# A two-layer graph network on one core: another order of the setup, and other buffers, banks and a queue for the adjacency

## The chip, the cores and the metric

The kernel runs on one core of one Trainium2 chip. The metric is the device time of one execution in microseconds (us); lower is better. A core has TensorE (PE; its weight loads are listed apart as PEld), VectorE (DVE), ScalarE (ACT), GpSimd (POOL) and SyncE (SP, here only a queue for DMAs). Each works through its own list of instructions in order, and semaphores make one wait for another.

## The reference

Eight graphs of 2048 nodes with 256 features share one 2048 x 2048 adjacency. Two layers follow each other; cut to what matters:

```python
# layer 0: h = relu(layernorm(x)); attention in 8 chunks of 256 keys, each with a softmax of its own
q, k, v = (h @ Wq.T + bq, h @ Wk.T + bk, h @ Wv.T + bv)       # 4 heads of 64
scores = clip(q . k / 8, -10, 10);  scores = where(adj == 0, -10, scores)
ctx = sum over chunks of softmax(scores in the chunk) @ v
x = x + layernorm(ctx @ Wo.T + bo + h) * gamma + beta
# layer 1: h = relu(layernorm(x)) again, called g here
h = g @ W;  e = leaky_relu(h . a1 [row] + h . a2 [column], 0.01)
x = x + relu(softmax(where(adj == 0, -1e9, e)) @ h)
```

## The kernel before

**Work.** The program is written out for each of the 8 graphs: a stretch of attention (32 steps: 4 blocks of 512 queries by 8 chunks of 256 keys), then the second layer. Before the first graph's attention stands a setup, once in the whole kernel; the changed code is in it, and in three helpers that it calls.

**Order.** `tc.manual_schedule` keeps the order of the source on all five engines, so the order of the calls is the order of each engine's list. A tile of a pool has a tag; a tag has a fixed number of buffers, and a new tile waits until a buffer's last user is done. A piece of work that waits holds up all that is behind it on its engine.

**Setup.** Four blocks of 512 rows of the first graph are loaded (`load`, SP), given statistics (`stats`, DVE), `power` (ACT) and `shift` (DVE: the last term of the norm), normed (`norm`, ACT, two halves), transposed (`turn`: TensorE, then a copy by DVE for half c = 0 and by ACT for c = 1), and projected: `qk(nb, 0)` gives q, `qk(nb, 1)` gives k (TensorE, then copies by ACT), `values` gives v (TensorE, then DVE). `turn_weight` transposes a weight on TensorE and copies it on DVE.

**Adjacency.** Beside that, the first 24 of the adjacency's 32 parts of 128 x 1024 are turned into "bounds", int8 values that serve as upper clip of the scores (the last 8 parts are done during the attention, by `adjacency`). For part i, `load_rows` brings 512 KB of int32 (four buffers; `find(i)` issues the load of part i + 4). `find` (`missing_of`, L211) compares with zero on DVE and gives z, in bf16. `bound` (`turn_missing`, L218, then `keep_bounds`) transposes z on TensorE in eight pieces to a bank of PSUM, and ACT scales it to int8. Parts 0 to 15 go to resident bounds of blocks 0 and 1; parts 16 to 23 go to a tile `bound_part`, and from there by a DMA of 128 KB to HBM (`bound_d`, runs of 128 bytes).

**PSUM.** Eight banks: tag "s" two tiles of two banks, "n" two of one bank, "t" two of one bank. In the setup `ps_m` takes "n" and "t" in turn, counting in `turn_about`; z's transposes take "t".

**SBUF tags that matter.** "hn" (5 buffers: normed halves, raw weights, and z), "e" (5: the attention's exponentials), "r" (2: `bound_part` in the setup; later a row of the second layer), "o4" and "prod" (1 each: output and product of the attention, both first used when the attention runs).

**The end of the setup.** `Attention.early` starts step 0 of the attention: part 0 the logits of its first two heads (they need block 0 of q and k alone), part 1 their clips (DVE) and exponentials (ACT) and the other heads' logits, part 2 clips, an exponential and a sum `add(0, 0)` of exponentials on GpSimd, part 3 the next step's first logits. After that `begin` and `end` run a step each: `begin(2)` holds the exponential of step 0's last head and `add(0, 1)`; `end(2)` holds the values matmuls (L427) and the sums matmuls (L439), which read both `add`s. On GpSimd's list stand these adds (L466) and, from the second chunk on, the DMAs that accumulate the context (L486). SP's list goes on, behind the setup's row loads, with the output weight (L190), the second layer's weight (L973), two stores of 1 MB of bounds (L129) and the next two parts' rows.

In the names of the setup, the loop before the change is:

```python
    for nb in range(NNB - 1):
        proj.norm(nb + 1, 0)
        proj.qk(nb, 0, ps_h)
        bound(6 * nb, 6 * nb + 1)
        proj.norm(nb + 1, 1)
        ...
        find(6 * nb + 2, 6 * nb + 3)
        proj.qk(nb, 1, ps_h)
```

Of the kernel before, what the change touches and what calls it, by code (L numbers as in the profile page):

```python
# [9 lines left out]
BF16 = mybir.dt.bfloat16  # L10
I32 = mybir.dt.int32
I8 = mybir.dt.int8
# [5 lines left out]
P = 128  # L18
# [10 lines left out]
def gnn_two_layers(  # L29
# [18 lines left out]
    nc = tc.nc  # L48
# [8 lines left out]
    NNB = N // NB  # L57
# [8 lines left out]
    ps = ctx.enter_context(tc.tile_pool(name="ps", bufs=2, space=PSUM))  # L66
# [11 lines left out]
    turn_about = [False, 0]  # L78

    def ps_m():  # L80
        if turn_about[0]:
            turn_about[1] += 1
            if turn_about[1] % 2:
                return ps_n()
        return ps_t()
# [8 lines left out]
    work = ctx.enter_context(tc.tile_pool(name="work", bufs=2, reuse_waits="tile"))  # L94
# [11 lines left out]
    wqT = const.tile([P, FC, F], F32, name="wqT")  # L106
    wkT = const.tile([P, FC, F], F32, name="wkT")
    wvT = const.tile([P, FC, F], F32, name="wvT")
# [6 lines left out]
    bound_d = [kept.tile([P, NT, NB], I8, name=f"bound_d{nb}") for nb in range(NNB)]  # L115
# [25 lines left out]
    def row_bcast(src, name):  # L141
        t = const.tile([P, F], F32, name=name)
        nc.sync.dma_start(t, row(src))
        return t
# [50 lines left out]
    def turn_weight(raw, wT):  # L195
        pt = ps_m()
        for di in range(FC):
            for do in range(FC):
                k = di * FC + do
                nc.tensor.transpose(pt[:, k * P:(k + 1) * P], raw[:, do, di * P:(di + 1) * P], ident)  # L200
        nc.vector.tensor_copy(wT.rearrange("p c f -> p (c f)"), pt)

    HALF = N // 2

    def load_rows(t, half):
        rows = xpool.tile([P, HALF], I32, tag="x", name="rows", bufs=NNB)
        nc.sync.dma_start(rows, adj[t * P:(t + 1) * P, half * HALF:(half + 1) * HALF])
        return rows

    def missing_of(rows, t, half):  # L210

        z = work.tile([P, HALF], BF16, tag="hn", name="z", bufs=5)
        nc.vector.tensor_scalar(
            z, rows, 0.0, 0.0, op0=ALU.is_equal, op1=ALU.add, accum_out=missing[:, t, half:half + 1]
        )
        return z

    def turn_missing(z):  # L218
        pt = ps.tile([P, 8, P], BF16, tag="t", name="ps_z")
        for k in range(8):  # L220
            nc.tensor.transpose(pt[:, k, :], z[:, k * P:(k + 1) * P], ident_b)
        return pt

    def keep_bounds(pt, t, half):

        nb, rows, cols = t // TB, slice(half * 8, (half + 1) * 8), slice((t % TB) * P, (t % TB + 1) * P)
        if nb in bounds:
            dst = bounds[nb][:, rows, cols]
        else:
            dst = work.tile([P, 8, P], I8, tag="r", name="bound_part")  # L230
        nc.scalar.activation(dst, pt, AF.Copy, scale=-2.0 * CLIP * SC, bias=CLIP * SC)
        if nb not in bounds:
            nc.scalar.dma_start(bound_d[nb][:, rows, cols], dst)

    def find_lone():
        nc.vector.tensor_reduce(lone, missing, AX.X, ALU.add)
# [4 lines left out]
    def adjacency(parts):  # L241


        def load(i):
            rows[i] = load_rows(*parts[i])

        def find(i):
            found[i] = missing_of(rows.pop(i), *parts[i])

        def turn(i):  # L250
            found[i] = turn_missing(found[i])

        def keep(i):
            keep_bounds(found.pop(i), *parts[i])

        finds = [9, 11, 15, 17, 21, 23, 29, 31]
        turns = [12, 12, 18, 18, 26, 26, 32, 32]
        todo = {}
        for i, (f, t) in enumerate(zip(finds, turns)):
            todo.setdefault(f - 6, []).append(lambda i=i: load(i))  # L260
            todo.setdefault(f, []).append(lambda i=i: find(i))
            todo.setdefault(t, []).append(pe(lambda i=i: turn(i)))
            todo.setdefault(t + 1, []).append(first(lambda i=i: keep(i)))
        return todo
# [628 lines left out]
    proj = Projection(0)  # L893
    turn_about[0] = True
    raws = {}
# [9 lines left out]
    rows = {i: load_rows(*nearest[i]) for i in range(4)}  # L905
    proj.stats(0, range(TB))
    proj.power(0)
    for name, wT in (("q", wqT), ("k", wkT), ("v", wvT)):
        turn_weight(raws[name], wT)
    proj.shift(0)  # L910
    proj.norm(0, 0)
    proj.norm(0, 1)
    proj.load(2)
# [4 lines left out]
    def find(*parts):  # L918
        for i in parts:
            found[i] = missing_of(rows.pop(i), *nearest[i])  # L920
            if i + 4 < len(nearest):
                rows[i + 4] = load_rows(*nearest[i + 4])

    def bound(*parts):
        for i in parts:
            keep_bounds(turn_missing(found.pop(i)), *nearest[i])

    find(0, 1)
    for nb in range(2):
        bounds[nb] = bound_tile()  # L930
    proj.stats(1, range(TB))
    proj.power(1)
    proj.shift(1)
    for nb in range(NNB - 1):
        proj.norm(nb + 1, 0)
        proj.qk(nb, 0, ps_h)
        bound(6 * nb, 6 * nb + 1)
        proj.norm(nb + 1, 1)
        if nb + 3 < NNB:
            proj.load(nb + 3)  # L940
        find(6 * nb + 2, 6 * nb + 3)
        proj.qk(nb, 1, ps_h)
        bound(6 * nb + 2, 6 * nb + 3)
        proj.turn(nb + 1, 0)
        proj.turn(nb + 1, 1)
        find(6 * nb + 4, 6 * nb + 5)
        if nb + 2 < NNB:
            proj.stats(nb + 2, range(TB))
            proj.power(nb + 2)
            proj.shift(nb + 2)  # L950
        proj.values(nb)
        bound(6 * nb + 4, 6 * nb + 5)
        if nb == 0:
            bo_r = row_bcast(bo, "bo_r")
            gamma_r = row_bcast(gamma, "gamma_r")
            beta_r = row_bcast(beta, "beta_r")
        find(6 * nb + 6, 6 * nb + 7)
    proj.qk(NNB - 1, 0, ps_h)
    att = Attention(proj)
    att.early(0)  # L960
    bound(18, 19)
    proj.qk(NNB - 1, 1)
    find(20, 21)
    att.early(1)
    bound(20, 21)
    find(22, 23)
    proj.values(NNB - 1)
    att.early(2)
    bound(22, 23)
    att.early(3)  # L970

    def layer1_weight():
        nc.sync.dma_start(w1s[:, :, 0:F], w1.rearrange("(c p) f -> p c f", p=P))  # L973
# [26 lines left out]
    for b in range(B):  # L1000
# [208 lines left out]
        for i, (nb, j4) in enumerate(pieces1):  # L1209
# [21 lines left out]
            if far and i in (1, 3, 6, 9):  # L1231
                n = (1, 3, 6, 9).index(i)
# [3 lines left out]
            if ahead and i == len(pieces1) - 4:  # L1236
                att = Attention(ahead)
# [38 lines left out]
```

## Time and profile before

| | us |
|---|---|
| median of 3 runs | 3614.5 |
| lowest, highest | 3611.58, 3620.66 |
| the profiled execution, whole | 3618.74 |
| its span, first to last instruction | 3616.9 |

| engine | busy us (share of the span) |
|---|---|
| PE | 3579.6 (99%) |
| DVE | 2583.1 (71%) |
| ACT | 1960.0 (54%) |
| POOL | 1787.0 (49%) |

The setup and the first step's start fill about the first 98 us of the span. In that stretch PE is busy for 76.89 us, DVE for 54.38, ACT for 51.82 and POOL for 3.23. A wait in the profile reads "who <- whom: total us, times, longest"; a row of a stretch gives its length, then the busy time of PE, PEld, DVE, ACT and POOL with the count of instructions, then the granted clock of TensorE, the DMA engines' share and GB/s.

### The profile page before, as it was taken

To read this page: it belongs to the slowest core of one execution; us is meant where nothing else is said; L and a number is where in the kernel's file an instruction comes from. 1 tells how busy PE (TensorE), PEld (TensorE's weight loads), DVE (VectorE), ACT (ScalarE), POOL (GpSimd) and SP (SyncE) were. 2 spreads that over 40 slices of the span, in tenths; PEclk is the share of its full clock that TensorE was granted. 3 is DMA by queue.
4 is the path that set the end of the run, shared out by engine and by line. 5 is a ranking of instruction groups with operands and counts; after the bars stand their busy time and mean duration, and the time that the engine had idled before them with its cause. 6 is when DMAs were issued, how large, how long until landed. Compare 5 with 4: busy or idle time off the path is not lost.

```text
span 3616.9 us, 104751 instructions
## 1 busy us (share of the span) xinstructions
PE 3579.6 (99%) x46544; PEld 2222.8 (61%) x46544; DVE 2583.1 (71%) x3919; ACT 1960.0 (54%) x2975; POOL 1787.0 (49%) x1138
## 2 busy tenths in 40 slices
PE   8999999999999999999999999999999999999999
PEld 4444785547855577555775558755586555865568
DVE  5888577865778667786677866677666785767866
ACT  5677416774167742677326772367723677137650
POOL 0678016870168702786027860378503784047841
PEclk9999999999999999999999999999999999999999
DMA  6444213341133412344113432134322343114321
GB/s 216 118 107 101 53 56 82 79 110 38 56 84 84 112 30 73 78 92 93 46 58 84 101 77 62 48 84 101 72 62 59 78 95 74 53 48 90 78 57 46
DMA packets 149430, 283.61 MB, mean 78 GB/s; under 512 B 39664, under 2 KB 104944, under 8 KB 140784
## 3 DMA queue, kind: packets, MB, share of 16 engines
q0 software_dynamic: 32256, 117.45, 17.7%
q1 hardware_dynamic: 100080, 157.36, 13.7%
q8 instruction: 364, 5.96, 0.7%
q10 hardware_dynamic: 16640, 2.10, 0.4%
q14 instruction: 90, 0.74, 0.1%
HBM read 138.41 MB, written 21.02 MB: 44 GB/s over the span
## 4 chain that ended last, share of the span: by engine, by line
PE 97%; DMA 1%; DVE 1%; ACT 1%; issue 0%; POOL 0%; ACTq 0%; SPq 0%; DVEq 0%; POOLq 0%
PE ps_s L411 24%; PE ps_n L427 24%; PE ps_s L856 12%; PE ps_t L439 6%; PE ps_n L856 6%; PE ps_t L856 6%; PE ps_t L635 2%; PE ps_t L355 2%; PE ps_n L355 2%; PE ps_s L355 2%; PE ps_n L714 2%; PE ps_t L714 1%; PE ps_t L369 1%; PE ps_n L369 1%; PE ps_t L302 1%; DMA ctxT<-prod 1%
## 5 line engine op out<-in xcount | busy, mean ns | idle before, releaser
L466 POOL TENSOR_TENSOR both<-e 128x1024 f32<-128x1024 f32 x512 | 1216.3, 2402 | 639.3 <-PE ps_t L439 340.8
L451 DVE SCALAR_TENSOR_TENSOR e<-ps_s,bound 128x1024 f32<-128x1024 f32 x1024 | 1225.0, 1221 | 412.1 <-PE ps_s L411 410.2
L411 PE MATMUL ps_s<-q,k 64*32 64x512 f32 x16384 | 1412.0, 590 | 2.1 <-DVE e L451 2.1
L460 ACT ACTIVATE e<-e 128x1024 f32<-128x1024 f32 x1024 | 1050.3, 1050 | 466.5 <-DVE e L451 447.9
L427 PE MATMUL ps_n<-e,v 64*32 64x512 f32 x16384 | 1206.8, 590 | 4.1 <-ACT e L460 2.2
L427 PEld LDWEIGHTS ps_n<-e,v 64*32 64x32 f32 x16384 | 456.6, 107 | 479.8 <-issue 397.2
L411 PEld LDWEIGHTS ps_s<-q,k 64*32 64x32 f32 x16384 | 454.2, 106 | 453.1 <-issue 343.9
L874 POOL TENSOR_TENSOR x<-x,r 128x256 f32<-128x256 f32 x124 | 95.7, 772 | 1104.1 <-DVE rz L866 997.3
L439 PE MATMUL ps_t<-both,ones 64*32 64x512 f32 x4096 | 534.6, 590 | 0.1
L856 PE MATMUL ps_s<-g,w 128*128 128x257 f32 x2048 | 447.3, 380 | 0.0
L856 PEld LDWEIGHTS ps_s<-g,w 128*128 128x128 f32 x2048 | 388.4, 190 | 56.0
L481 DVE TENSOR_TENSOR prod<-ps_n,rz 128x512 f32<-128x512 f32 x448 | 288.7, 686 | 166.3 <-PE ps_n L427 96.6
L839 DVE SCALAR_TENSOR_TENSOR w<-bound,w 128x1024 f32<-128x1024 int8 x256 | 313.7, 1225 | 8.7
L856 PE MATMUL ps_n<-g,w 128*128 128x257 f32 x1024 | 292.4, 382 | 0.0
L856 PE MATMUL ps_t<-g,w 128*128 128x257 f32 x1024 | 289.7, 380 | 0.0
L471 ACT ACTIVATE rz<-ps_t 128x512 f32<-128x512 f32 x256 | 152.6, 596 | 229.8 <-PE ps_t L439 185.7
L833 DVE TENSOR_SCALAR w<-src,cd 128x512 f32<-128x512 f32 x512 | 265.3, 561 | 10.7 <-ACT src L827 6.9
L486 POOL DMA_DIRECT2D ctxT<-prod x224 | 192.3, 859 | 57.8 <-DVE prod L481 55.5
L856 PEld LDWEIGHTS ps_n<-g,w 128*128 128x128 f32 x1024 | 192.8, 190 | 44.3 <-issue 17.6
L856 PEld LDWEIGHTS ps_t<-g,w 128*128 128x128 f32 x1024 | 193.8, 189 | 28.2
L275 ACT ACTIVATE krn<-mv,eps 128x4 f32<-128x4 f32 x32 | 9.5, 296 | 292.7 <-DVE mv L271 292.7
L472 ACT ACTIVATE rz<-rz 128x512 f32<-128x512 f32 x256 | 161.4, 630 | 8.2
(125 smaller groups left out, 2953.3 us busy)
## 6 DMA issues: line engine op xcount, KB each, us to landing
ctxT<-prod POOLq DMA_DIRECT2D x224, 512.0 KB, 4.8
bound<-bound_d SPq DMA_DIRECT2D x62, 1024.0 KB, 5.7
xp<-in_x_dram SPq DMA_DIRECT2D x60, 512.0 KB, 5.7
rows<-in_adj_dram SPq DMA_DIRECT2D x32, 512.0 KB, 5.2
x<-in_x_dram SPq DMA_DIRECT2D x32, 512.0 KB, 5.3
out_dram<-x SPq DMA_DIRECT2D x31, 512.0 KB, 2.9
src<-source_d SPq DMA_DIRECT2D x24, 256.0 KB, 5.0
bound_d<-bound_part ACTq DMA_DIRECT2D x16, 128.0 KB, 4.3
```

The lines of the kernel that those rows point to most:

```text
L355: nc.tensor.matmul(pp, w[:, di, do * P:(do + 1) * P], self.hT[nb][:, di, :], start=di == 0, stop=di == FC - 1,)
L411: nc.tensor.matmul(self.s[n, o][c * Q:(c + 1) * Q, kt, :], self.k[p][rows, at:at + Q], self.q[p][rows, nb * NB:(nb + 1) * NB], start=True, ...
L427: made.append(nc.tensor.matmul(self.num[n, c][h * Q:(h + 1) * Q, :], self.v[rows, j * KT + kt, at:at + Q], self.e[n, p][rows, i * KT + kt, :],
L439: nc.tensor.matmul(self.total[n][h * Q:(h + 1) * Q, :], ones[rows, :], self.both[n, h // 2][rows, h % 2, :], start=half == 1, stop=half == 0,)
L451: nc.vector.scalar_tensor_tensor(self.e[n, p][:, i * KT:(i + 1) * KT, :], self.s.pop((n, o)), -CLIP * SC, bounds[nb][:, j * KT:(j + 1) * K ...
L460: nc.scalar.activation(e, e, AF.Exp, scale=1.0 / SC)
L466: nc.gpsimd.tensor_tensor(self.both[n, p], e[:, 0], e[:, 1], op=ALU.add)
L481: nc.vector.tensor_tensor(dst[:, c, :], self.num.pop((n, c)), self.rz[n], op=ALU.mult)
L486: nc.gpsimd.dma_start(self.ctxT[nb], self.prod.pop(n), accum_op=ALU.add)
L833: nc.vector.tensor_scalar(w[:, i, :], self.src[nb], self.cd[:, 0, j:j + 1], self.cd[:, 1, j:j + 1], op0=ALU.mult, op1=ALU.max,)
L839: nc.vector.scalar_tensor_tensor(two, bounds1[nb][:, j - 1:j + 1, :], 0.0, two, op0=ALU.is_gt, op1=ALU.mult)
L856: nc.tensor.matmul(accs[t][:, 0:F + 1], w[:, i, t * P:(t + 1) * P], g[:, j, :], start=j == 0, stop=j == NT - 1,)
```

## The change

- In the setup z is put in a buffer of tag "e" and not "hn" (`in_setup`, set to False when the setup is written out).
- A bound that goes to HBM takes a buffer of tag "r", "o4", "r" or "prod" by part: parts 16, 18, 20, 22 "r" (two buffers), 17 and 21 "o4", 19 and 23 "prod". Its DMA is issued from GpSimd and not from ACT.
- While `turn_about` is on, z's transposes take "n" and "t" in turn, in one count with `ps_m`.
- The order: block 0's `shift` stands ahead of the copies of the k and v weights; block 1's statistics and shift stand ahead of finds 0 and 1; in the loop, finds stand ahead of bounds, both norms of a block stand one block earlier behind the transposes (block 1's after q of block 0), the next block's statistics ahead of the transposes; `early(0)` stands ahead of block 3's q, which now takes "n" and "t"; the values of block 3 stand behind all bounds.

```diff
@@ -201,6 +201,9 @@
         nc.vector.tensor_copy(wT.rearrange("p c f -> p (c f)"), pt)
 
     HALF = N // 2
+    in_setup = [True]
+
+    part_tags = ["r", "o4", "r", "prod"]
 
     def load_rows(t, half):
         rows = xpool.tile([P, HALF], I32, tag="x", name="rows", bufs=NNB)
@@ -209,14 +212,20 @@
 
     def missing_of(rows, t, half):
 
-        z = work.tile([P, HALF], BF16, tag="hn", name="z", bufs=5)
+        tag = "e" if in_setup[0] else "hn"
+        z = work.tile([P, HALF], BF16, tag=tag, name="z", bufs=5)
         nc.vector.tensor_scalar(
             z, rows, 0.0, 0.0, op0=ALU.is_equal, op1=ALU.add, accum_out=missing[:, t, half:half + 1]
         )
         return z
 
     def turn_missing(z):
-        pt = ps.tile([P, 8, P], BF16, tag="t", name="ps_z")
+        tag = "t"
+        if turn_about[0]:
+            turn_about[1] += 1
+            if turn_about[1] % 2:
+                tag = "n"
+        pt = ps.tile([P, 8, P], BF16, tag=tag, name="ps_z")
         for k in range(8):
             nc.tensor.transpose(pt[:, k, :], z[:, k * P:(k + 1) * P], ident_b)
         return pt
@@ -227,10 +236,12 @@
         if nb in bounds:
             dst = bounds[nb][:, rows, cols]
         else:
-            dst = work.tile([P, 8, P], I8, tag="r", name="bound_part")
+            tag = part_tags[(2 * t + half) % 4] if in_setup[0] else "r"
+            dst = work.tile([P, 8, P], I8, tag=tag, name="bound_part", bufs=2 if tag == "r" else 1)
         nc.scalar.activation(dst, pt, AF.Copy, scale=-2.0 * CLIP * SC, bias=CLIP * SC)
         if nb not in bounds:
-            nc.scalar.dma_start(bound_d[nb][:, rows, cols], dst)
+            queue = nc.gpsimd if in_setup[0] else nc.scalar
+            queue.dma_start(bound_d[nb][:, rows, cols], dst)
 
     def find_lone():
         nc.vector.tensor_reduce(lone, missing, AX.X, ALU.add)
@@ -905,9 +916,10 @@
     rows = {i: load_rows(*nearest[i]) for i in range(4)}
     proj.stats(0, range(TB))
     proj.power(0)
-    for name, wT in (("q", wqT), ("k", wkT), ("v", wvT)):
-        turn_weight(raws[name], wT)
+    turn_weight(raws["q"], wqT)
     proj.shift(0)
+    turn_weight(raws["k"], wkT)
+    turn_weight(raws["v"], wvT)
     proj.norm(0, 0)
     proj.norm(0, 1)
     proj.load(2)
@@ -925,49 +937,54 @@
         for i in parts:
             keep_bounds(turn_missing(found.pop(i)), *nearest[i])
 
-    find(0, 1)
     for nb in range(2):
         bounds[nb] = bound_tile()
     proj.stats(1, range(TB))
     proj.power(1)
     proj.shift(1)
+    find(0, 1)
     for nb in range(NNB - 1):
-        proj.norm(nb + 1, 0)
+        i = 6 * nb
         proj.qk(nb, 0, ps_h)
-        bound(6 * nb, 6 * nb + 1)
-        proj.norm(nb + 1, 1)
-        if nb + 3 < NNB:
-            proj.load(nb + 3)
-        find(6 * nb + 2, 6 * nb + 3)
+        if nb == 0:
+            proj.norm(1, 0)
+            proj.norm(1, 1)
+            proj.load(3)
+        find(i + 2, i + 3)
+        bound(i, i + 1)
         proj.qk(nb, 1, ps_h)
-        bound(6 * nb + 2, 6 * nb + 3)
-        proj.turn(nb + 1, 0)
-        proj.turn(nb + 1, 1)
-        find(6 * nb + 4, 6 * nb + 5)
+        find(i + 4, i + 5)
+        bound(i + 2, i + 3)
         if nb + 2 < NNB:
             proj.stats(nb + 2, range(TB))
             proj.power(nb + 2)
             proj.shift(nb + 2)
+        proj.turn(nb + 1, 0)
+        proj.turn(nb + 1, 1)
+        if nb + 2 < NNB:
+            proj.norm(nb + 2, 0)
+            proj.norm(nb + 2, 1)
         proj.values(nb)
-        bound(6 * nb + 4, 6 * nb + 5)
+        find(i + 6, i + 7)
+        bound(i + 4, i + 5)
         if nb == 0:
             bo_r = row_bcast(bo, "bo_r")
             gamma_r = row_bcast(gamma, "gamma_r")
             beta_r = row_bcast(beta, "beta_r")
-        find(6 * nb + 6, 6 * nb + 7)
-    proj.qk(NNB - 1, 0, ps_h)
     att = Attention(proj)
     att.early(0)
+    proj.qk(NNB - 1, 0)
+    att.early(1)
+    find(20, 21)
     bound(18, 19)
     proj.qk(NNB - 1, 1)
-    find(20, 21)
-    att.early(1)
+    att.early(2)
     bound(20, 21)
     find(22, 23)
+    bound(22, 23)
     proj.values(NNB - 1)
-    att.early(2)
-    bound(22, 23)
     att.early(3)
+    in_setup[0] = False
 
     def layer1_weight():
         nc.sync.dma_start(w1s[:, :, 0:F], w1.rearrange("(c p) f -> p c f", p=P))
```

## The prediction

> **What bounds the kernel now.** I read the page's first two parts first, then stretches by engine, then waits and the chain inside the first 100 us.
>
> ```profile
> PE 3579.6 (99%) x46544; PEld 2222.8 (61%) x46544; DVE 2583.1 (71%) x3919; ACT 1960.0 (54%) x2975; POOL 1787.0 (49%) x1138
> PE   8999999999999999999999999999999999999999
> ```
>
> TensorE is busy in every slice but the first. So only the first slice, where the changed code runs, can move: what TensorE saves there is saved at the end, and nothing else is. I cut that slice at the starts of the four q projections and of the first values matmul that runs on (98.5), with 200 us of the later work below:
>
> ```profile
> 13.15:34.50 21.35, 16.74 (x89) 10.66 (x89) 13.49 (x34) 11.54 (x21) 0.00 (x0) 0.98 0.69 237
> 34.50:53.40 18.90, 15.72 (x91) 10.08 (x89) 10.61 (x24) 11.48 (x18) 0.00 (x0) 0.93 0.53 179
> 53.40:70.20 16.80, 16.00 (x92) 10.13 (x90) 9.01 (x17) 10.11 (x15) 0.00 (x0) 0.90 0.48 159
> 70.20:98.50 28.30, 22.68 (x200) 10.68 (x196) 16.41 (x22) 14.63 (x17) 2.35 (x1) 1.00 0.81 222
> 200.00:400.00 200.00, 199.96 (x3231) 104.01 (x3218) 151.24 (x231) 148.19 (x234) 140.70 (x91) 1.00 0.40 92
> ```
>
> Columns: length, then busy time of PE, PEld, DVE, ACT, POOL, then TensorE's clock, DMA share, GB/s. No engine is full in the four stretches; in-order waits make them long. TensorE's waits from 13 to 98.6, and two of the others:
>
> ```profile
> PE ps_z L221 <- DVE v L374: 4.8, 2, 2.4
> PE ps_t L302 <- ACT bound L231: 2.4, 3, 0.8
> PE ps_n L427 <- ACT e L460: 2.2, 1, 2.2
> PE ps_s L411 <- DVE e L451: 2.1, 2, 1.1
> PE ps_s L355 <- ACT q L359: 1.4, 1, 1.4
> ACT krn L275 <- DVE mv L271: 17.6, 4, 5.1
> ```
>
> The first: a second transpose of the adjacency needs bank "t" of the value that VectorE has not yet read, since VectorE stands behind finds and statistics. The last stretch, from the chain:
>
> ```profile
> 84.44 1.02 ACT bound_part L231
> 85.46 0.02 issue
> 85.48 8.85 DMA bound_d<-bound_part
> 94.33 0.02 issue
> 94.35 0.02 ACTq L231
> ```
>
> A bound leaves for HBM through one of two buffers; the next waits for the landing (8.85 us), and the exponentials stand behind it on ScalarE.
>
> **What the skill says.** "TensorE: Matmul & The Clock Gate", Part 1: idleness halves the clock, and some microseconds of work restore it. The trace agrees: after the 2.4 us waits the q matmuls start 0.85 apart and not 0.43, at clock 0.93 and 0.90 above. "SBUF — State Buffer", Who interferes with whom: `tensor_scalar` with an accumulator does not lock GpSimd out. The finds are that form, 1.22 us for 1024 elements; no run here shows it beside a GpSimd DMA. "DMA: Bandwidth & Descriptors", Anatomy of one DMA: GpSimd's descriptor generation is "small, variable". "Perfetto Trace Analysis", DMA Instruction — SWDGE: the profiled GpSimd DMA ends when its descriptors are written. The trace has that for one shape alone:
>
> ```profile
> L486 POOL DMA_DIRECT2D ctxT<-prod x224: 815/858/986, 118.0 to 3474.3; - x112
> ```
>
> **The change, step by step.** Durations from the timeline (us): TensorE: four transposes 0.42, q or k of a block 3.45 (first q 4.85, at half clock), half a block's values 1.7, one adjacency part 0.45, two heads' logits 1.72. ScalarE: two bounds 1.93, two q or k copies 1.25, hT 0.6, four norms 2.07, power 0.8, exponential 1.05. VectorE: find 1.14, a block's statistics 2.13, hT 0.69, v 0.68, clip 1.18.
>
> *Start.* shift(0) runs ahead of the k and v weights' copies: it needs only the power, done at 7.93. Norms start at 8.15, not 9.77; q(0) at 11.55, not 13.15: **1.6**. The extra wait of the two copies is 0.2 us, in front of an idle engine.
>
> *Block 0.* Statistics of block 1 (x lands 12.11) 12.15 to 14.3, its shift to 15.2, finds 0 and 1 to 17.5: later than before by 1.6, and so are SP's row loads 4, 5. But ScalarE takes q before norms: q copied by 17.3, norms to 19.4, bounds 0 and 1 to 21.35, k to 22.6, bounds 2 and 3 to 24.5. TensorE: q to 16.4, parts 0 and 1 to 18.0, k to 21.5 (its banks are free by 17.3), parts 2 and 3 to 22.4, hT's transposes to 23.3, values (banks after bounds 2, 3) 23.5 to 26.9, parts 4, 5 to 27.8. hT is copied by 26.1. q(1) at 27.8: 16.3 long, not 21.35: **5.0**. The clock stays up.
>
> *Block 1.* The values' banks and hT's copy have come (v copied 26.8 and 27.8, hT 40.0, before TensorE asks at 40.9). Load 3 on SP waits for the norms (19.4) and holds rows 6, 7 to about 25; finds 6, 7 run from 27.8. Rows 10, 11 are issued when those finds free them, land by 34.3 (4 us, as the median 5.2 allows), and their parts are needed at 35.7 on. TensorE's own work: q and k 6.9, parts 6 x 0.45, hT 0.85, values 3.4: 13.9; with 0.1 for a bound, 14.0, not 18.9: **4.9**.
>
> *Block 2.* The same 14.0, against 16.8: **2.8**. q(3) of before (70.2) corresponds to 55.8.
>
> *End.* TensorE: logits of heads 0 and 1 to 57.5 (block 3 not needed), q(3) 60.95, logits 62.7, parts 18, 19 63.6, k(3) 67.05, parts 20 to 23 69.3, values 69.95 to 73.4 (banks after bounds 20, 21), next step's logits to 77.9. Before, those logits ended at 96.3 and the values ran on at 98.5 because the exponential had waited for bounds. Here ScalarE ends bound 23 at 72.8 if no buffer is late and the exponential at 73.9. So 22.2 against 28.3: **6.1**.
>
> *Finds in the exponentials' buffers.* Live at once at most five: parts 18 to 21 and one e. A find then waits for a part's transpose; the worst, find 23, waits for part 20 (67.5), costing VectorE 0.8 us with 1 us in hand before part 23 would be missed. Banks of both kinds: a fifth allocation waits, not a third; it is in the sums.
>
> *Bounds by GpSimd, four buffers.* ScalarE loses eight issues of 0.37 to 0.42, 3.1 us, in the End's 1 us of slack. SP's list is unchanged, but the output weight, two 1 MB stores and two row loads now start at 58 and not 77.6, beside parts 18, 19. Their landing took 4.2 to 8.85 before; issued at 65.5 and 66.5 they free buffers for bounds 22, 23 between 70 and 75.5, when asked for at 71 and 72: a stall of 0 to 3.6, of which TensorE sees at most 2 (exponential at 77.5).
>
> GpSimd's new work is the unknown, d per DMA. Each part is 1040 packets (128 bytes each), its context DMA 144:
>
> ```profile
> q0 software_dynamic: 32256, 117.45, 17.7%
> q10 hardware_dynamic: 16640, 2.10, 0.4%
> ```
>
> (32256/224; 16640/16.) Lower bound: 0.86, if descriptors are free as the skill's sentence has it. Upper: in proportion, 0.86 x 1040/144 = 6.2. No gain below 0.86 is possible: the same instruction. Behind these DMAs on GpSimd stand add(0,0), then add(0,1) of 2.36 each, which the sums matmuls read. From bound 16 (56.5) both are done at the latest at 56.5 + 8d + 4.7, and from bound 18 at 64.75 + 6d + 4.7. TensorE wants them at 80.5. With d up to 1.8 nothing is lost. I take 1.5, nearer the lower end because part of 0.86 must be fixed.
>
> Sum: 1.6 + 5.0 + 4.9 + 2.8 + 6.1 = 20.4, less about 2.4 for a late bound buffer and the 0.05 to 0.2 us of each release that I rounded: **18.0**. The profiled execution is 3618.7 (span 3616.9), 0.1% above the median of 3614.5; 3616.9 - 18 = 3598.9 of span, 3600.7 with its launch, and **3596.5** as a median. The later code is unchanged and bound by TensorE.
>
> **Rivals.** What this kernel's measurement can tell from no change is 0.3%, 10.8 us.
>
> 1. *Forecast*, 0.62: gain 15 to 22, 3592 to 3600.
> 2. *Descriptors cost GpSimd 2.5 to 5 us*, 0.20: sums become ready at 61.2 + 8d: d = 3 gives 85.2, a gain of 15.9 less rounding, some 13, 3601; d = 4 gives 93.2, gain about 7, 3607. For it: eight times the packets. Against it: the skill's sentence.
> 3. *Dearer still: GpSimd becomes the bound of the end and it is slower*, 0.08. Before, the sums ran at 101.1. 61.2 + 8d reaches that at d = 5.0, the deciding point; at 6.2 it is 110.8, 9.7 us later: 3624. With bounds 22, 23 also waiting for landings and exponentials behind them, over 0.3% is within reach. For it: proportion to packets is the plainest reading. Against it: it needs 0.86 to have no fixed part.
> 4. *The savings turn into new waits*, 0.10: rows late in each block. VectorE's finds are the only ones without a full block of lead; if each of SP's pairs lands at the slow 9.3 us (seen at the start and at 84), three blocks lose 3 to 4 us each: gain 8, 3607. Against it: DMA moves 159 to 237 GB/s in these blocks, and 358 from 10 to 20 us.
>
> That the change doesn't act: moving instructions in the hand-written order acts by itself; only the e buffers could keep old waits, and then the 4.8 us stay: inside 1 and 4.
>
> **Numbers.** Over 0.3% faster: rival 1 and most of 2 (d under 3.6), a quarter of 4: 0.62 + 0.13 + 0.03 = 0.78. Within: rest of 2 and 4, half of 3: 0.14. Slower: 0.08, rounded up for what I don't see. Range 3589 (all 20.4 plus 2 us of restored clock after 98.5, and 3 us of run-to-run spread) to 3608 (rivals 2 and 4).
>
> **What would show it.** q projections starting near 11.6, 28, 42 and 57.5 us; no wait of a transpose for DVE v; clock 1.0 from 17 us on; no bound_part wait for a DMA over 4 us; TensorE continuous from about 79 us, not 98.5. GpSimd's eight DMA rows of 1 to 2 us. Wrong, if these rows exceed 3.6 us and sums wait for "both", or if the finds wait for rows.

## The result, and the profile after

The changed kernel takes 3596.23 us (median of 6 runs, 3593.45 to 3603.5) against 3618.81 for the kernel before in the same comparison (6 runs, 3611.58 to 3621.7): ratio 0.9942, 95% interval 0.9933 to 0.9952. In a second comparison it took 3596.32 against 3613.73, ratio 0.9946 (0.9933 to 0.9959). It is faster by about 0.55%; the forecast was 3596.5. The profiled execution's span fell from 3616.9 to 3595.5, by 21.4.

The page of the changed kernel, parts 1 and 2:

```profile
PE 3574.0 (99%) x46544; PEld 2230.5 (62%) x46544; DVE 2582.9 (72%) x3919; ACT 1959.7 (55%) x2975; POOL 1793.6 (50%) x1146
PE   9999999999999999999999999999999999999999
```

The counts of instructions are the same, but for GpSimd's eight new DMAs, and every engine's busy time is within 8 us of before. Of the 21.4 us, 15.8 are idle time of TensorE that went; the other 5.6 are busy time, and most of that (4.25) went in the three blocks, where fewer matmuls now run at a lower clock. The first slice reads 9 too. The same slice, cut as before at the q projections of blocks 0, 1 and 2, at the first logits (56.15; they now stand ahead of block 3's q) and shortly before the first values (78.56); columns are the length, busy PE, PEld, DVE, ACT, POOL, then TensorE's clock, DMA share, GB/s:

```profile
11.47:27.38 15.91, 15.59 (x89) 9.96 (x89) 12.75 (x33) 11.89 (x23) 0.00 (x0) 1.00 0.91 326
27.38:41.87 14.49, 14.34 (x91) 9.50 (x89) 10.97 (x25) 11.27 (x19) 0.00 (x0) 1.00 0.75 265
41.87:56.15 14.28, 14.28 (x92) 9.50 (x89) 9.31 (x17) 9.66 (x14) 0.00 (x0) 1.00 0.66 223
56.15:77.70 21.55, 19.52 (x178) 10.05 (x180) 14.04 (x19) 13.90 (x17) 10.70 (x10) 1.00 0.85 267
```

PE's busy time nearly equals the length in the three blocks, and the granted clock is 1.00 where it was 0.93 and 0.90. TensorE's waits from 11 to 100 us:

```profile
PE ps_s L422 <- DVE e L462: 1.3, 1, 1.3
PE ps_z L230 <- DVE z L217: 0.7, 2, 0.4
PE ps_t L380 <- ACT bound_part L241: 0.2, 1, 0.2
PE ps_z L230 <- DVE hT L352: 0.2, 1, 0.2
```

2.4 us are left, and the largest of the old ones (a transpose waiting for `DVE v`) is gone. The start of the first context DMA on GpSimd is a mark for the length of the setup: the code after it is the same in all kernels here but the two whose stores are moved. It moved by 20.8 us, from 118.0:

```profile
L497 POOL DMA_DIRECT2D ctxT<-prod x224: 809/852/932, 97.2 to 3451.4; - x112
```

So 20.8 of the span's 21.4 us lie in the setup. A mark comes from one execution. Two executions of the changed kernel gave 97.2 and 97.7. The kernel before is less steady: in two kernels below that leave its block code as it was, the fourth q starts at 67.3 and 69.0, not at 70.2, so some 1 to 3 us of a difference to 118.0 can be chance. Behind the mark one execution differs from the next, too: from the mark to the end, the twelve traces with the same code there take 3495.4 to 3502.4 us. Ratios and marks are both given below for that reason.

### The profile page after: what moved, and what is told of

The parts are those of the page before. It is cut to its first block, busy times and chain, and to the rows that moved or that the text cites. A ratio compares the mean times of both kernels' runs of the same rounds, so it can differ in the third digit from the quotient of the medians.

```text
span 3595.5 us, 104747 instructions
## 1 busy us (share of the span) xinstructions
PE 3574.0 (99%) x46544; PEld 2230.5 (62%) x46544; DVE 2582.9 (72%) x3919; ACT 1959.7 (55%) x2975; POOL 1793.6 (50%) x1146
## 3 DMA queue, kind: packets, MB, share of 16 engines
q10 hardware_dynamic: 8320, 1.05, 0.2%
## 4 chain that ended last, share of the span: by engine, by line
PE 97%; DVE 1%; DMA 1%; ACT 1%; POOL 0%; issue 0%; DVEq 0%; ACTq 0%; POOLq 0%
PE ps_s L422 25%; PE ps_n L438 24%; PE ps_s L867 12%; PE ps_t L450 6%; PE ps_n L867 6%; PE ps_t L867 6%; PE ps_t L646 2%; PE ps_t L366 2%; PE ps_n L366 2%; PE ps_s L366 2%; PE ps_t L725 2%; PE ps_t L380 2%; PE ps_n L725 2%; PE ps_n L380 1%; PE ps_t L313 1%; DMA ctxT<-prod 1%
## 5 line engine op out<-in xcount | busy, mean ns | idle before, releaser
L497 POOL DMA_DIRECT2D ctxT<-prod x224 | 190.9, 852 | 57.1 <-DVE prod L492 48.7
```

Source lines behind the costliest of these rows:

```text
L497: nc.gpsimd.dma_start(self.ctxT[nb], self.prod.pop(n), accum_op=ALU.add)
```

## Experiments: each part left out, each part alone

The mark shows where the time goes, in one execution; the ratio shows what a part is worth in time, over 5 to 12 runs of each kernel (0.0010 is 3.6 us). For most kernels the mark shows the larger saving: for the banks alone 11.8 us against 5 by the ratio (2 to 8), for the four buffers alone 6.2 against none that can be told. Differences of a few us in the mark are therefore not a measure of the time. "Fourth q" is the start of block 3's q projection, "logits" that of the attention's first logits.

| kernel | fourth q / logits | mark | ratio to before (95%) |
|---|---|---|---|
| before | 70.2 / 73.8 | 118.0 | 1 |
| order alone | 60.8 / 58.9 | 113.9 | 0.9997 (0.9989 to 1.0006) |
| banks alone | 59.9 / 63.5 | 106.2 | 0.9986 (0.9978 to 0.9995) |
| four buffers alone | 67.3 / 70.9 | 111.8 | 0.9998 (0.9990 to 1.0006) |
| order and banks | 58.3 / 56.4 | 104.5 | 0.9971 (0.9960 to 0.9982) |
| all but the order | 59.7 / 63.3 | 101.6 | 0.9966 (0.9954 to 0.9979) |
| all but the banks | 60.4 / 58.5 | 105.2 | 0.9971 (0.9961 to 0.9981) |
| all but four buffers | 58.3 / 56.4 | 103.5 | 0.9965 (0.9956 to 0.9975) |
| all but GpSimd's queue | 59.0 / 57.1 | 100.8 | 0.9953 (0.9937 to 0.9970) |
| all but the e buffers | 58.0 / 56.1 | 97.1 | 0.9958 (0.9946 to 0.9970) |
| changed | 58.0 / 56.1 | 97.2 | 0.9942 (0.9933 to 0.9952) |

### All but the order

The changed kernel with the old sequence of calls in the setup:

```diff
-        i = 6 * nb
+        proj.norm(nb + 1, 0)
         proj.qk(nb, 0, ps_h)
...
-        find(i + 2, i + 3)
-        bound(i, i + 1)
+        bound(6 * nb, 6 * nb + 1)
+        proj.norm(nb + 1, 1)
...
+    proj.qk(NNB - 1, 0, ps_h)
     att = Attention(proj)
     att.early(0)
```

> The changed kernel with the setup in its old order; the e buffers, the banks of both kinds, the four bound buffers and GpSimd's queue stay. Mark of the setup's length: the first context DMA on GpSimd (118.0 us before, 97.2 changed). Theory (the order brings most, by keeping ScalarE and VectorE ahead of TensorE): the landing wait and the bank waits of 4.8 us are gone, the rest stays, so the mark is near 110 and the time about 8 us under the kernel before. Rival (the buffers and banks bring most): the mark is under 103, at most 6 us behind the changed kernel.

Measured: mark 101.6. By the mark the rival is right: with buffers, banks and queue, the old order is only 4.4 us behind. By the ratios it is 8.7 us behind, with intervals of some 4 us to each side, so the rival's limit of 6 stays open. Its blocks take 47.2 us together (12.5 to 59.7), against 57.05 before and 44.7 changed.

### Order alone

The kernel before with the new sequence of calls (the reverse of the diff above, and nothing in the helpers). 

> The kernel before with only the setup's new order: z in hn, z's transposes in bank t alone, two bound buffers, bounds issued by ScalarE. Theory: the order alone takes the three blocks' and the start's 10 to 13 us; at the end bounds wait for landings through two buffers and cost 3 to 5 us. Mark near 106, about 12 us under the kernel before. Rival (order alone cannot act, since two banks t hold up the transposes): mark over 112.

Measured: mark 113.9, and the time cannot be told from before. The rival's number is met, but not for its reason: the blocks do run (fourth q at 60.8, and 1.9 us of logits already done), and the end takes it back. TensorE's largest wait from 13 to 100 us:

```profile
PE ps_t L369 <- ACT bound_part L231: 8.1, 1, 8.1
```

Two stretches at the end of the same kernel, with TensorE's clock third from the right:

```profile
60.70:77.00 16.30, 12.45 (x104) 6.21 (x96) 9.53 (x14) 9.81 (x12) 2.36 (x1) 0.99 0.85 235
77.00:91.00 14.00, 6.39 (x16) 4.92 (x16) 0.69 (x1) 3.10 (x3) 2.35 (x1) 0.53 0.55 138
```

In the new order block 3's values stand behind all bounds and need a bank "t" that bound 22 must leave; bound 22 waits for the landing of bound 20 (9.1 us) in its one of two buffers. TensorE waits for 8.1 us, and the values that follow run at half clock: they take 6.5 us, not 3.65 as in the changed kernel, and the clock column of the second stretch reads 0.53. The early blocks had only brought TensorE to this landing sooner.

### Banks alone

```diff
-        pt = ps.tile([P, 8, P], BF16, tag="t", name="ps_z")
+        tag = "t"
+        if turn_about[0]:
+            turn_about[1] += 1
+            if turn_about[1] % 2:
+                tag = "n"
+        pt = ps.tile([P, 8, P], BF16, tag=tag, name="ps_z")
```

> The kernel before with z's transposes in banks of both kinds and nothing else. Theory (in the blocks the banks and the order stand in for each other: TensorE waits there for a bank whose reader is late, which goes with more banks or with earlier readers): the fourth q starts near 60 us, as with the order alone (60.8), against 70.2; the end is then set by the landings of bounds 18 to 21 through two buffers, and the mark is 108 to 113. Rival (the blocks' gain needs all parts): fourth q at 65 or later.

Measured: fourth q at 59.9, mark 106.2 (a little better than expected). In the blocks the banks and the order stand in for each other: either alone brings the fourth q about 10 us forward, and in the changed kernel, with both, the block stretch is 12.4 shorter (57.05 to 44.68; 44.89 with order and banks and nothing else). In the kernel before, TensorE waited there for a bank of tag "t" with a late reader. More banks make the lateness harmless; an order that puts the reader earlier removes it. At the end the landing still rules, as the chain shows:

```profile
73.22 1.02 ACT bound_part L236
74.24 0.02 issue
74.26 8.22 DMA bound_d<-bound_part
82.48 0.02 issue
```

### All but the banks

```diff
         tag = "t"
-        if turn_about[0]:
-            turn_about[1] += 1
-            if turn_about[1] % 2:
-                tag = "n"
         pt = ps.tile([P, 8, P], BF16, tag=tag, name="ps_z")
```

> The changed kernel with z's transposes in bank t alone. Theory: the third use of t waits for the second last reader, and values wait for bounds: some 1 us a block, 3 to 5 us in all, mark 100 to 102. Rival (the new order alone keeps the readers ahead): mark within 1 us of 97.2.

Measured: mark 105.2, more than either expected. Fourth q is 2.3 us late; the rest is the end, where first values start at 86.6 and not 78.6. Bound 18 leaves 2.3 us later (67.88), its landing takes 8.1, and block 3's values, again tied to bound 22 through bank "t", wait for it. With two kinds of banks the values wait for bounds 20 and 21, which need no late landing. Under the new order the banks are thus worth most at the end, by parting the values from bounds 22 and 23.

### Four buffers: left out, and alone

```diff
-    part_tags = ["r", "o4", "r", "prod"]
+    part_tags = ["r", "r", "r", "r"]
```

> The changed kernel with two bound buffers (all bounds that go to HBM in r), issued by GpSimd. Theory: bounds 20 and 21 wait for the landings of 18 and 19 (72.6 and 74.4), 22 and 23 for those of 20 and 21 (some 78 and 79), the last exponential starts near 81 and not 75.4, values matmuls near 82 and not 78.6: mark 100 to 101. Rival (the landing waits of before were the whole of the end's loss): mark 103 or more. Other rival (nothing waits on it): 97.

Measured: mark 103.5. ScalarE's largest wait from 52 to 100 us:

```profile
ACT bound_part L241 <- DMA bound_d<-bound_part: 6.1, 4, 3.3
```

Four waits, at 73.3, 75.1, 77.4 and 79.2, as expected one behind the other; the last exponential starts at 80.1. What the expectation left out is that block 3's values wait 3.6 us for bound 20's bank, so TensorE's first values come at 84.8, not 82.

Alone, on the kernel before:

```diff
-            dst = work.tile([P, 8, P], I8, tag="r", name="bound_part")
+            tag = ["r", "o4", "r", "prod"][(2 * t + half) % 4] if nb == 2 else "r"
+            dst = work.tile([P, 8, P], I8, tag=tag, name="bound_part", bufs=2 if tag == "r" else 1)
```

> The kernel before with four bound buffers (r, o4, r, prod), still issued by ScalarE, and nothing else. Theory: fourth q at 70.2 as before; bounds 22 and 23 wait for the landings of 18 and 19 (82.4, 83.4 before), not of 20 and 21 (94.3, 95.0), so the wait of 8.85 us for a landing goes, and VectorE's clips and the logits, 91 to 98 us, remain: mark 113 to 115. Rival (the landing wait was the whole of the end): mark 109.

Measured: mark 111.8, and no bound waits for a landing any more. The block code is unchanged, yet fourth q came 2.9 us earlier in this execution, so about 3.3 of the 6.2 us belong to the buffers, in the range of the theory; the ratio shows no difference.

### All but GpSimd's queue

```diff
-            queue = nc.gpsimd if in_setup[0] else nc.scalar
+            queue = nc.scalar
```

> The changed kernel with the eight bounds' DMAs issued by ScalarE as before; order, buffers and banks stay. Theory: eight issues of 0.37 to 0.42 us go back to ScalarE, 3.1 us, of which the part between bound 20 and the last exponential (four issues, 1.6 us) is seen at most: mark 97 to 99. Rival (GpSimd's packets cost something that hid): mark under 97, faster.

Measured: mark 100.8, above the expectation. One microsecond is chance of the start: the first q took 6.1 us, not 4.66, k began 1.0 us later, and so did the first logits (57.1 against 56.1). The rest is ScalarE's list at the end:

```profile
71.70 2.27 ACTq L244 DMA_DIRECT2D bound_d<-bound_part  x1
74.02 1.02 ACT L241 ACTIVATE bound_part<-ps_z 128x1024 int8<-128x1024 bf16 x1 [2.35 <-PE ps_t L380]
75.07 2.75 ACTq L244 DMA_DIRECT2D bound_d<-bound_part  x1
78.19 1.02 ACT L241 ACTIVATE bound_part<-ps_z 128x1024 int8<-128x1024 bf16 x1 [3.15 <-DMA bound_d<-bound_part]
```

With four buffers ScalarE issues the DMAs of bounds 20 and 21 while two and three earlier ones are still in flight, and these issues hold ScalarE for 2.27 and 2.75 us, not 0.37. The trace names PE for the first gap, but the row ahead of it is the issue. What bound 22 waits for in the end is the landing of bound 18, which left at 66.27, and the chain goes through it:

```profile
66.27 11.83 DMA bound_d<-bound_part
```

In the changed kernel that landing took 7.0 us. The last held issue ends at 77.8 and the landing at 78.1, so either alone would have kept bound 22 about as long. The queue's worth is thus not 1.6 us of issue time, but held issues and a later landing. The two queues also cut the same bytes into different packets (1040 from ScalarE's, 48 from GpSimd's; the lines stand with the forecast of d, further down), and no run separates that from the engine that issues. By the marks, leaving out the buffers or the queue costs 6.3 or 3.7 us, and leaving out both (next) 7.3, less than the sum. By the ratios it is 8, 4 and 10 us, with intervals of 3 to 6 us to each side, which leaves the sum open.

### Order and banks alone

The kernel of "order alone" with the diff of "banks alone".

> The kernel before with the new order and z's banks of both kinds; two bound buffers, ScalarE's queue and hn stay. Theory (the blocks need order or banks, the end needs the four buffers and the queue, which act on one wait, the landing of bounds 18 and 19): the fourth q and first logits start as in the changed kernel (58.0 and 56.1), and the mark is late by the sum of what leaving out either cost, 6.3 and 3.7 us, or more, 107 to 111. Rival (the two are worth no more together than the larger alone): mark 103 to 104.

Measured: mark 104.5, between the two. Blocks are those of the changed kernel (44.9 us), first values start at 78.8 as in it, and then TensorE waits 5.3 us for the last exponential, which stands behind an 8.6 us wait for a landing. By the mark the rival is nearer: it is one wait that buffers and queue act on.

### All but the e buffers

```diff
-        tag = "e" if in_setup[0] else "hn"
+        tag = "hn"
```

> The changed kernel with z in the hn buffers, as before. Theory: a block has two normed halves and up to four z, six tiles for five buffers; a find then waits for one transpose of an earlier part, which TensorE has done by then or does within 1 us: mark within 1 us of 97.2. Rival (the waits of finds for transposes, 4.6 us before, come back and reach TensorE): mark 100 or more.

Measured: mark 97.1, as in the changed kernel. The ratios, 0.9958 and 0.9942, have intervals that overlap only a little (0.9946 to 0.9952). A cost of a few us is not excluded by them, but the setup's trace shows none.

### Who makes the landing slow

SP's two stores of 1 MB moved from the attention's piece 2 to 10 (a piece is a numbered place between its instructions where other work is put in), in the kernel before:

```diff
-        2: [lambda: store_bounds(0), lambda: store_bounds(1)],
+        10: [lambda: store_bounds(0), lambda: store_bounds(1)],
```

> The kernel before with SP's two stores of bounds (1 MB each) at the attention's piece 10 and not 2, all else as before. Theory (a bound's landing is slow because it shares the DMA engines with what SP sends at that time): the landing of bound 20, 8.85 us, falls to 5 or less, and the mark to 113 to 115. Rival (1024 runs of 128 bytes are slow by themselves): landing over 7 us, mark within 1 us of 118.

Measured: bound 20 lands in 3.3 us and 21 in 2.5, not 8.85 and 8.0, so the slowness is that of the traffic beside it, here of the two stores, as the theory said. In the trace of bound_part, 80 to 90 us:

```profile
DMA to landing us min/median/max: 2.5/2.9/3.3
```

The mark is 113.6, with 1.2 of the 4.4 us from an earlier fourth q, but the ratio is 0.9998 (0.9990 to 1.0007). The stores come back later, at 115.5 and between context DMAs, and TensorE waits there:

```profile
PE ps_n L427 <- DVE prod L481: 1.5, 1, 1.5
```

That is less than the mark gained; where the rest of it goes is not shown.

### An attempt at a faster one

The changed kernel, plus:

```diff
+            for i in range(TB):
+                nc.sync.dma_start(t[:, i, :], rows4[:, i, :])
...
+    for i in range(18):
+        nc.tensor.transpose(warm[:, 0, (i % 4) * P:(i % 4 + 1) * P], ident, ident)
...
-        2: [lambda: store_bounds(0), lambda: store_bounds(1)],
+        10: [lambda: store_bounds(0), lambda: store_bounds(1)],
```

> The changed kernel with three additions: the two stores at piece 10, the first x block loaded in four DMAs of a tile each, and 18 transposes of the identity on TensorE ahead of the first weight (their result is read by nobody) so that its clock is up. Theory: no landing wait at the end (1 to 2 us), the first q 1 to 1.5 us earlier by the statistics and at full clock (4.66 to 3.65 us): mark 93 to 95, time 2 to 4 us under the changed kernel. Rival (the start is bound by what stands behind it, rows among them): mark within 1 us of 97.2.

Measured: mark 98.9, 3605.96 us, ratio 0.9974 (0.9963 to 0.9984): slower than the changed kernel. The first q ran at full clock (3.70 us; 4.66 and 3.93 in the changed kernel's two executions) and began at 11.15, but what follows it was not ready. The two longest of TensorE's waits from 5 to 560 us:

```profile
PE ps_z L235 <- DVE z L222: 2.5, 3, 1.5
PE ps_n L443 <- DVE prod L497: 2.2, 2, 1.7
```

Two stretches around the gap, in the same columns as above:

```profile
11.00:16.40 5.40, 3.70 (x9) 1.44 (x9) 3.55 (x13) 2.54 (x7) 0.00 (x0) 1.00 1.02 381
16.40:23.00 6.60, 6.08 (x24) 3.25 (x25) 4.52 (x8) 4.24 (x7) 0.00 (x0) 0.74 0.90 272
```

Find 0 stands behind block 1's statistics, and their x landed at 11.94, no earlier than in the changed kernel (10.81 and 11.79 in its two executions). So TensorE came sooner to a z that did not come sooner. With the gap the clock dropped (0.74), and k took 4.89 us, not 3.65. Around the late stores TensorE waited 2.2 us in the attention. These waits do not make up the whole difference in time to the changed kernel; the rest is not located. No version here beats the changed kernel.

### The changed kernel again

No edit.

> The changed kernel again, beside the run above and more runs of the kernel before, since medians of single parts stood 3 to 6 us from what their marks said. Theory: the gain is the mark's, 20 to 22 us, ratio 0.9939 to 0.9945, and the spread of runs is half-clock stretches later in the kernel that do not depend on the setup. Rival: the gain is smaller, 15 to 18 us.

Measured: mark 97.7, a gain of 20.3 as the theory has it. The ratio is 0.9946 (0.9933 to 0.9959), a gain of 19.5 us in an interval from 15 to 24, and the medians are 17.4 apart. So the time decides for neither: the ratio lies just short of the theory's range, and the medians' difference in the rival's. Part of the spread arises behind the setup (the 3495.4 to 3502.4 us above); that it is made of stretches at half clock is not shown.

## Why the prediction was right, point by point

- *TensorE alone counts, and only in the first slice.* Right: 20.8 of 21.4 us of span.
- *Start, 1.6.* The first q came at 11.47, 1.68 earlier. Part of it is chance of the kernel before: the others with the old start have it at 12.4 to 12.7, so the new start is worth some 1 us against those. In the old start the norms stand behind the v weight, which landed at 7.78 before and at 6.99 in "all but the order" (q at 12.47); in the second execution of the changed kernel it landed at 8.65, and q still came at 11.52.
- *Blocks, 16.3, 14.0 and 14.0.* Measured 15.91, 14.49 and 14.28: together 12.4 saved where 12.7 was forecast. TensorE's own work is 14.3, not 13.9 (PE column above).
- *End, 22.2 against 28.3.* First values at 78.56 after logits at 56.15: 22.4, so 5.9 saved where 6.1 was forecast.
- *A late bound buffer, 0 to 3.6 us on ScalarE, at most 2 on TensorE.* Bound 22 waited 1.1 us for a landing (3.3 in two waits in the second execution); TensorE waited 0.2 for bound_part. *Find 23* waited 0.9 us (0.8 forecast), and TensorE 0.4 for its z.
- *GpSimd's d, 0.86 to 6.2, taken as 1.5.* Measured 0.89 to 1.09, from the rows of bound_part in the changed kernel:

```profile
L244 POOL DMA_DIRECT2D bound_d<-bound_part x8: 887/887/1094, 57.1 to 75.8; - x8
```

The first ran beside a find (from 57.10), which took its usual 1.22 us. So the lower end was the right one, and with it rivals 2 and 3 fell. But the reason on which they stood, 1040 packets for each of these DMAs, was not put to the test. It was read from ScalarE's queue (q10). In the page of the changed kernel, part 3:

```profile
q0 software_dynamic: 32640, 118.50, 17.9%
q10 hardware_dynamic: 8320, 1.05, 0.2%
```

GpSimd's queue (q0) has 384 packets more than before for the eight DMAs, 48 each, of 2.7 KB on average; q10 has 8320 fewer. So the same 128 KB went in 48 packets and not in 1040. A DMA of 48 packets took 0.89 us on GpSimd and the context DMA's 144 take 0.85: between these two the price does not go with the packets. What 1040 would have cost, and how many descriptors GpSimd wrote for its 48, no run shows. "DMA: Bandwidth & Descriptors" (Anatomy of one DMA) of the Trainium skill calls the cost of generating descriptors "small, variable"; 0.89 us for a bound agrees with small. The forecast didn't depend on it: by its own sum, anything up to 1.8 us was free.
- *Rival 4, rows late.* Finds waited 3.9 us for rows, 3.1 of it ahead of find 17, which ended at 52.2 and was not needed before 55.2. TensorE waited 0.7 us for z.
- *The deduction of 2.4 us was not needed.* The steps, 20.4 by the working, came to 20.0 in the traces (first values at 78.56, not 98.51), and the mark moved by 20.8. TensorE's waits for bound buffers and its idle time in the three blocks, for which the 2.4 us stood, came to 0.2 and 0.5. So 18.0 was low by 3, inside the range. That the median came within 0.3 us of the forecast is luck: the forecast took 3614.5 for the kernel before, which came out at 3618.8 beside it and at 3613.7 to 3615.7 in the other comparisons.

What the working did not see is how the parts share the gain. It counted the blocks' 12.7 us under the order. The runs show that the banks alone bring most of that (blocks of 47.2 us, against 54.9 to 57.05 with the old code), that the order alone brings nothing that can be measured in the time, and that it needs the banks and buffers because it moves the values behind the bounds.

## What to carry to other kernels

When an engine waits for a buffer of a ring with a late reader, more buffers and an earlier reader are two cures for one wait: cost them together, not as a sum. Follow a saving to the next thing that stands on another clock, here a DMA's landing: work that arrives there sooner only waits longer, and if the wait is long TensorE then runs at half clock. A store that is in the way in a slack stretch may still be in its best place if the later stretch has none.

## What the hardware showed that I had not expected

- A bound's 128 KB (1024 runs of 128 bytes) went in 1040 packets from ScalarE's queue and in 48 from GpSimd's. The DMA held GpSimd for 0.89 us (1.09 the first), the context's, with 144 packets, for 0.85.
- A DMA issue on ScalarE took 0.37 us usually, but 2.27 and 2.75 with two and three of its DMAs still in flight beside SP's traffic. What it waited for inside, the trace doesn't tell.
- The 128 KB of a bound (runs of 128 bytes) landed in 2.1 to 2.7 us when SP's stores were done, and in 7 to 11.8 beside SP's stores and row loads at their slowest.
- Waits of 1.5 and 0.5 us in a busy stretch were followed by a stretch at lower clock (0.74); waits of 0.8 and 0.5 at the same place, in the second execution of the changed kernel, were not (k in 3.65 us). An 8.1 us wait was followed by 6.5 us of values at half speed. "TensorE: Matmul & The Clock Gate" (Part 1) of the Trainium skill names an idle window of about 3.4 us for the half clock; here shorter waits did it.
